# Four-layer graph network on one core: target rows and the scan's zero in a PSUM bank, sort steps pinned behind the messages, half runs as row groups in layer 2

## The chip, the cores and the metric

The kernel runs on one core of one Trainium2 chip. The core has five engines that run side by side and meet at semaphores: TensorE (PE in the profile, its weight loads PEld), VectorE (DVE), ScalarE (ACT), GpSimd (POOL) and SyncE (SP), which here only issues DMAs. SBUF is the working memory of 128 partitions; PSUM is a smaller memory of banks that TensorE writes and VectorE and ScalarE read. The metric is device time in microseconds (us); lower is better.

## The reference

A graph has 6250 nodes with 160 numbers each (64 scalars, 32 vectors of three components) and 100000 edges, sorted by their target node `dst`. Four layers follow one another, and each adds its result to the node rows:

```python
h = jnp.maximum(_layernorm(x, axis=-1), 0.0)
x = x + _L0_gnn_ref(h, node_vec1, src, dst, edge_attr_4, edge_attr_12, ...)
# the same frame for layers 1, 2 and 3; inside layers 0, 1 and 3:
h0, h1 = node-wise linear maps of h                  # scalars and vectors
w      = silu(edge_features @ W_fc1) @ W_fc2         # 192 weights for each edge
e0, e1 = h0[edge_src], h1[edge_src]                  # gather by source
mid_s  = concat(w0 * e0 * y0, w3 * dot(e1, y1))
mid_v  = concat((w1 * e0)[:, :, None] * y1[:, None, :], w2[:, :, None] * (e1 * y0))
ns, nv = segment_sum(mid_s, edge_dst), segment_sum(mid_v, edge_dst)
out    = node-wise linear maps of ns, nv, plus a linear map of h
```

Layer 2 has the directions turned around: it takes its node rows by `dst` and sums by `src`. Its messages must therefore be sorted by source first.

## The kernel before

Edges are handled in tiles of 128 (one edge per partition), four tiles to a group (`G = 4`), 28 tiles to a unit `u`, two windows of `WT = 14` tiles to a unit. There are 784 tiles (`TT`), 196 groups and 56 windows (`NW`) in every layer. A window's 14 tiles are two half runs of seven tiles, interleaved, so that tiles of even number belong to the first half and tiles of odd number to the second; each half touches fewer than 64 target nodes (`HN = 64`).

The program is `prologue()`, then `layers()`: `edges(0)`, `edges(1)`, `messages2()` and `sums2()` for layer 2, `edges(3)`. The order of instructions on each engine follows the order in which the Python code issues them, as a scheduler with a model of the engines rearranges it: an instruction that it sees ready may move ahead of earlier code that it sees waiting.

**Layers 0, 1 and 3 (`edges`).** For every group: `gather` (L1277) issues four indirect DMAs on POOL, each of which fetches 128 table rows by source into the tile `ge` (eight buffers, issued six groups ahead). `hidden` and `edge_weights` make the 192 weights per edge (matmuls L1266 or L1260, then L1300 or L1293; ScalarE evicts at L1304 and L1306 into `ws`). `messages` on VectorE makes the one-hot `oh` of targets (L1319: `iota` compared with `loc`) and the messages `msg` (L1330 to L1338). The matmul L1394 adds them up by target in the PSUM tile `pg`. At the end of a window, `nodes` takes the sums through `nodes_out` and `nodes_in` of the next layer, in small steps between the groups.

The tile `yls` (L1226) lies in a PSUM bank that VectorE alone uses. At the first group of a unit, L1313 copies three columns of the edges' directions into it, and L1330 and L1337 read them from there. The targets' rows `self.loc` are read from SBUF by L1319.

**The sort.** `positions()` is a generator that works out where each edge goes in source order: for each of the 54 buckets `b`, it makes `hit` (L1166), a running count `cum` with `tensor_tensor_scan` (L1168; its second input is `self.zeros_b`, a row of 784 zeros in SBUF), then multiplies (L1171) and adds into `pos` (L1172). Four steps come before the buckets, two steps belong to each bucket, one comes last. In layers 0 and 1, every third group asks for one step:

```python
            if li < 2 and i % 3 == 0:
                next(self.sort, None)
```

That is 66 steps in each of the two layers, of which 113 are needed.

**Layer 2, first part (`messages2`).** `select(k)` loads for window `k` 128 rows of the node table from the window's first node on (`tb`, L1443) and the targets of its 1792 edges, repeated on all partitions (`dt`, L1445, 896 KB), both through SP's queue; VectorE compares `dt` with each partition's node number `plus_w` (L1447) into the one-hot `oh`. In `messages`, the matmul L1479 (K = 128) picks each edge's row into the PSUM tile `pe`; ScalarE copies it out (L1484 to L1486); VectorE makes the message rows (L1497 to L1506); POOL scatters each tile's 128 rows to their sorted places in `rec2` (L1509; `row` has five buffers). `sums2` then reads `rec2` in order and adds up by source (L1611, L1613).

Of the kernel before, what the change touches and what calls it, by code (L numbers as in the profile page):

```python
# [11 lines left out]
F32 = mybir.dt.float32  # L12
BF16 = mybir.dt.bfloat16
I32 = mybir.dt.int32
AF = mybir.ActivationFunctionType
ALU = mybir.AluOpType
# [4 lines left out]
N = 6250  # L21
E = 100000
P = 128
# [9 lines left out]
G = 4  # L33
# [656 lines left out]
class Fast:  # L690
# [16 lines left out]
    def prologue(self):  # L707
# [119 lines left out]
        nc.tensor.matmul(pw[:, 2, :], lhsT=self.ones[0:1, :], rhs=wd[:, 3, :], start=True, stop=True)  # L827
        nc.vector.tensor_scalar(self.plus_w, pw[:, 0, :], iota_p, None, op0=ALU.add)

        column = pro.tile([P, NW], F32, name="column0")  # L830
        nc.vector.tensor_scalar(column, pw[:, 1, :], place, None, op0=ALU.add)
        other = pro.tile([P, NW], F32, name="other")
        nc.vector.tensor_tensor(other, column, pw[:, 2, :], ALU.not_equal)
# [308 lines left out]
    def positions(self, wk):  # L1142
# [21 lines left out]
        for b in range(BK + 1):  # L1164
            hit = wk.tile([P, TT], BF16, name="hit2", bufs=2)
            nc.vector.tensor_scalar(hit, self.src_b, float(b), None, op0=ALU.is_equal)  # L1166
            cum = wk.tile([P, TT], F32, name="cum", bufs=2)
            nc.vector.tensor_tensor_scan(cum, hit, self.zeros_b, self.off[:, b : b + 1], op0=ALU.add,  # L1168
                                         op1=ALU.add)
            yield  # L1170
            nc.vector.tensor_mul(cum, cum, hit)  # L1171
            nc.vector.tensor_add(pos, pos, cum)  # L1172
            yield
# [25 lines left out]

    def at(self, k, most=N):  # L1200

        return self.nc.values_load(self.first[0:1, 2 * k : 2 * k + 1], engines=[mybir.EngineType.SP], min_val=0, max_val=most,
                                   skip_runtime_bounds_check_because="a node's number")

    def edges(self, li):
# [19 lines left out]

        yls = p_y.tile([P, 2, 3, 2 * WT], F32, name="yls")  # L1226

# [81 lines left out]
        def messages(u, g):  # L1309
            n = width(u, g)  # L1310
            rt, yl = data[u][0], yls[:, u % 2]
            if g == 0:
                nc.vector.tensor_copy(yl, rt[:, :, 1:4].rearrange("p t c -> p c t"))  # L1313
            ws = wss.pop((u, g))[:, :n]
            ge = gath.pop((u, g))[:, :n]
            gs = slice(G * g, G * g + n)
            oh = wk.tile([P, G, HN], F32, name="oh", bufs=3)
            t0 = 2 * WT * u + G * g
            tt(oh[:, :n], self.iota[:, None, :HN].to_broadcast([P, n, HN]),  # L1319
               self.loc[:, t0 : t0 + n, None].to_broadcast([P, n, HN]), ALU.is_equal)  # L1320
            msg = wk.tile([P, G, AW + 64], F32, name="msg", bufs=3)[:, :n]
            mvec = msg[:, :, 0:288].rearrange("p g (c m) -> p g c m", c=3)
            e0 = ge[:, :, 0:64]
            e1 = ge[:, :, 64:160].rearrange("p g (c u) -> p g c u", c=3)
            yv = yl[:, :, gs].rearrange("p c t -> p t c")
            t1 = msg[:, :, AW : AW + 64]
# [10 lines left out]
            tt(mvec[:, :, :, 0:64], by3(t1, 64), yv[:, :, :, None].to_broadcast([P, n, 3, 64]), ALU.mult)  # L1337
            tt(mvec[:, :, :, 64:96], e1, by3(ws[:, :, 64:96], 32), ALU.mult)  # L1338
            return oh, msg

# [41 lines left out]
        for i, (u, g) in enumerate(groups):  # L1382
            prepare(i + AHEAD)
            weights_of(i + 2)
            if i + 1 < len(groups):
                edge_weights(*groups[i + 1])
            oh, msg = messages(u, g)
            for k in range(width(u, g)):
# [12 lines left out]
            if li < 2 and i % 3 == 0:  # L1401
                next(self.sort, None)
        for n in live:
# [7 lines left out]
    def messages2(self):  # L1411
# [26 lines left out]
        def select(k):  # L1438

            n = min(WT, TT - WT * k) * P  # L1440
            at = self.at(k)
            tb = ld.tile([P, 160], F32, name="tb")
            nc.sync.dma_start(tb, self.table[2][ds(at, P), :])  # L1443
            dt = ld.tile([P, WT * P], I32, name="dt", bufs=2)
            nc.sync.dma_start(dt[:, :n], self.a["dst_w"][k : k + 1, :n].to_broadcast([P, n]))  # L1445
            oh = ld.tile([P, WT, P], F32, name="oh", bufs=3)
            nc.vector.tensor_scalar(oh.rearrange("p t e -> p (t e)")[:, :n], dt[:, :n], self.plus_w[:, k : k + 1], None,  # L1447
                                    op0=ALU.is_equal)
            ohs[k] = tb, oh
# [22 lines left out]
        def messages(u, g):  # L1472
            n = width(u, g)
            t0 = 2 * WT * u + G * g
            ts = slice(t0, t0 + n)
            pe = p_e.tile([P, G, 256], F32, name="pe")
            for k in range(n):
                tb, oh = ohs[(t0 + k) // WT]
                nc.tensor.matmul(pe[:, k, :160], lhsT=oh[:, (t0 + k) % WT, :], rhs=tb, start=True, stop=True)  # L1479
            pw = pws.pop((u, g))[:, :n]  # L1480
            pe = pe[:, :n]
            row = wk.tile([P, G, RW], F32, name="row", bufs=5)[:, :n]
            ev = wk.tile([P, G, 224], F32, name="ev", bufs=3)[:, :n]
            nc.scalar.copy(ev[:, :, 0:160], pe[:, :, 0:160])  # L1484
            nc.scalar.copy(ev[:, :, 160:224], pe[:, :, 64:128])
            nc.scalar.copy(row[:, :, 294:390], pe[:, :, 64:160])  # L1486
            nc.scalar.copy(row[:, :, 256:262], self.edge_in[:, ts, :])
# [165 lines left out]
def _layout(inputs):  # L1653
# [46 lines left out]
    a["dst_t"] = by_tile(i["dst"], 1 << 20).T  # L1700
    a["dst_w"] = by_tile(i["dst"], 1 << 20).reshape(NW, WT * P)
    rec0 = np.zeros((E, 8), np.float32)
# [58 lines left out]
```

## Time and profile before

| | us |
|---|---|
| median of 3 runs | 6616.68 |
| the three runs | 6699.25, 6581.44, 6616.68 |
| the profiled execution, whole | 5448.67 |
| its span, first to last instruction | 5446.9 |

The profiled execution took 1168 us less than the median of the runs without a profile. What follows is about the profiled one; the stages are cut at the first and last indirect DMA of each:

| stage | us | what it is |
|---|---|---|
| 0 to 171 | 171 | prologue |
| 171 to 1265 | 1094 | gathers of layer 0 |
| 1265 to 1324 | 59 | from layer 0 to layer 1 |
| 1324 to 2395 | 1071 | gathers of layer 1 |
| 2395 to 2455 | 60 | from layer 1 to layer 2 |
| 2455 to 3550 | 1095 | scatters of layer 2 |
| 3550 to 4380 | 830 | sums of layer 2 |
| 4380 to 5420 | 1040 | gathers of layer 3 |
| 5420 to 5447 | 27 | end |

How to read it: "busy" of an engine is the time its instructions took, and a busy engine need not be the one that sets the end. An indirect DMA on POOL is an instruction in which POOL prepares the transfer; the transfer itself comes after it. "Idle before" is the time in which the engine had nothing running, put down to what ended it; "issue" means that the profile shows nothing that was waited for.

### The profile page before, as it was taken

The numbers are of one execution on the slowest core, as the hardware profiler recorded it, in microseconds if no ns is written. First come the engines' busy times: TensorE is split into PE (matmuls) and PEld (weight loads), VectorE is DVE, ScalarE is ACT, GpSimd is POOL, SyncE is SP. The second block draws the span as 40 slices with busy tenths as digits, with TensorE's granted clock in tenths as the row PEclk, the third lists the DMA queues.
The fourth block names the chain that finished last, engine by engine and source line by source line (L and its number), as shares of the span: only waits on it lengthen the run. The fifth ranks groups of instructions, "written<-read, shape, count | busy, mean of one in ns | idle before, by whom it ended". The sixth has DMA issues, their size and how long they took to land.

```text
span 5446.9 us, 77043 instructions
## 1 busy us (share of the span) xinstructions
PE 4624.0 (85%) x22084; PEld 2866.7 (53%) x22084; DVE 4217.8 (77%) x11655; ACT 2087.1 (38%) x6858; POOL 3346.0 (61%) x3143
## 2 busy tenths in 40 slices
PE   6799999997999999976666666689999988888887
PEld 4455555554555555544444444478888844444443
DVE  6688889888878897867777777767777767777777
ACT  5344444443544444533333333312222243343433
POOL 0577777774777777747777777700000067777776
PEclk9899999998989898987787877799999978788887
DMA  3333333322333333336666666477777533333332
GB/s 95 105 97 88 91 87 90 88 75 73 98 94 94 90 95 93 90 101 239 215 219 215 222 218 223 166 283 237 238 235 237 164 87 80 82 81 82 83 79 57
DMA packets 371211, 733.89 MB, mean 135 GB/s; under 512 B 69677, under 2 KB 249098, under 8 KB 370650
## 3 DMA queue, kind: packets, MB, share of 16 engines
q1 hardware_dynamic: 207122, 379.11, 22.3%
q0 software_dynamic: 163072, 349.43, 22.0%
q8 instruction: 180, 2.95, 0.2%
q14 instruction: 253, 2.07, 0.1%
q10 hardware_dynamic: 584, 0.33, 0.0%
HBM read 519.59 MB, written 209.08 MB: 134 GB/s over the span
## 4 chain that ended last, share of the span: by engine, by line
PE 52%; DVE 16%; DMA 14%; POOL 6%; issue 5%; ACT 3%; SPq 0%; DVEq 0%; ACTq 0%; POOLq 0%
PE pg L1394 12%; PE pg L1613 7%; DMA rec<-row,edge_to 7%; PE pw L1300 7%; DMA ge<-table,rt 6%; PE pg L1611 5%; POOL ge L1277 5%; PE ph L1266 4%; PE pa L1022 3%; PE pt_out L1062 2%; PE po L1082 2%; POOL rec L1509 2%; PE ph L1455 2%; DVE msg L1337 2%; PE pw L1293 2%
## 5 line engine op out<-in xcount | busy, mean ns | idle before, releaser
L1277 POOL DMA_INDIRECT ge<-table,rt x2352 | 2489.1, 1058 | 1774.1 <-DMA skip<-sk 830.3
L1394 PE MATMUL pg<-msg,oh 128*64 128x384 f32 x4704 | 1061.4, 572 | 165.6 <-DVE msg L1338 139.7
L1509 POOL DMA_INDIRECT rec<-row,edge_to x784 | 856.1, 1092 | 299.0 <-issue 191.2
L1304 ACT ACTIVATE ws<-pw,rt 128x96 f32<-128x96 f32 x2352 | 695.8, 348 | 820.5 <-DVE msg L1338 298.6
L1300 PE MATMUL pw<-w_w2y,hh 100*128 100x192 f32 x3136 | 673.5, 353 | 10.6 <-ACT ws L1306 7.7
L1394 PEld LDWEIGHTS pg<-msg,oh 128*64 128x64 f32 x4704 | 305.9, 150 | 709.0 <-issue 252.5
L1300 PEld LDWEIGHTS pw<-w_w2y,hh 100*128 100x128 f32 x3136 | 534.9, 202 | 236.9 <-ACT ws L1306 138.6
L1337 DVE TENSOR_TENSOR msg<-msg,yls 128x768 f32<-128x768 f32 x588 | 555.7, 945 | 0.0
L1613 PE MATMUL pg<-msg,oh 128*120 128x288 f32 x1668 | 541.5, 406 | 0.0
L1330 DVE TENSOR_TENSOR pr<-ge,yls 128x384 f32<-128x384 f32 x588 | 320.2, 545 | 220.7 <-DMA ge<-table,rt 219.9
L1269 ACT ACTIVATE hh<-ph 100x1024 f32<-100x1024 f32 (+1 forms) x336 | 269.1, 801 | 463.7 <-PE pw L1293 206.2
L1479 PE MATMUL pe<-tb,oh 128*128 128x160 f32 x1568 | 348.4, 363 | 112.5 <-ACT row L1486 112.3
L1266 PE MATMUL ph<-ft,w_w1r 12*100 12x512 f32 (+1 forms) x784 | 382.3, 658 | 71.2 <-ACT hh L1269 57.0
L1611 PE MATMUL pg<-rt,oh 128*120 128x192 f32 x1668 | 410.0, 328 | 29.3 <-DMA rt<-rec 29.3
L1479 PEld LDWEIGHTS pe<-tb,oh 128*128 128x128 f32 x1568 | 277.6, 226 | 274.5 <-ACT row L1486 221.9
L1333 DVE TENSOR_TENSOR msg<-ws,ge 128x512 f32<-128x512 f32 x588 | 402.0, 684 | 0.0
L1306 ACT COPY ws<-pw 128x192 f32<-128x192 f32 x1176 | 388.5, 330 | 0.0
L1455 PE MATMUL ph<-ft,w_w1d 128*128 128x512 f32 x224 | 162.4, 819 | 263.2 <-ACT hh L1457 262.4
L1502 DVE TENSOR_TENSOR row<-pw,ev 128x512 f32<-128x512 f32 x196 | 135.2, 690 | 301.8 <-ACT row L1488 298.3
L1611 PEld LDWEIGHTS pg<-rt,oh 128*120 128x120 f32 x1668 | 298.0, 184 | 117.6 <-issue 30.7
L1331 DVE TENSOR_REDUCE dot<-pr 128x128 f32<-128x384 f32 x588 | 344.2, 585 | 0.1
L1338 DVE TENSOR_TENSOR msg<-ge,ws 128x384 f32<-128x384 f32 x588 | 324.4, 552 | 0.0
(486 smaller groups left out, 7327.6 us busy)
## 6 DMA issues: line engine op xcount, KB each, us to landing
rt<-rec SPq DMA_DIRECT2D x208, 780.0 KB
dt<-in_dst_w_dram SPq DMA_DIRECT2D x56, 896.0 KB
ge<-table,rt POOLq DMA_INDIRECT x2352
ft<-in_ft_dram SPq DMA_DIRECT2D x56, 512.0 KB
ft<-in_ft_dram SPq DMA_DIRECT2D x28, 896.0 KB
xt<-x SPq DMA_DIRECT2D x168, 82.0 KB
rec<-row,edge_to POOLq DMA_INDIRECT x784
rt<-in_rec_dram SPq DMA_DIRECT2D x84, 112.0 KB
```

Of the source, the lines that this page charges most:

```text
L1266: nc.tensor.matmul(ph[:, i], lhsT=w1[r : r + K, :], rhs=ft[r : r + K, 4 * P * (j // 2) :][:, : 4 * P], start=True, stop=True)
L1277: nc.gpsimd.indirect_dma_start(out=ge[:, k, :], out_offset=None, in_=self.table[li], in_offset=bass.IndirectOffsetOnAxis(ap=rt[:, G * g + ...
L1300: nc.tensor.matmul(pw[:, i, :192], lhsT=hh[:, k + i, :], rhs=w2, start=True, stop=True)
L1304: nc.scalar.activation(ws[:, k0 + i, 0:96], pw[:, i, 0:96], AF.Copy, scale=rt[:, G * g + k0 + i, 0:1])
L1306: nc.scalar.copy(ws[:, k0 : k0 + m, 96:192], pw[:, :m, 96:192])
L1333: tt(msg[:, :, AW - 64 : AW + 64].rearrange("p g (k u) -> p g k u", k=2), ws.rearrange("p g (k u) -> p g k u", k=2)[:, :, :, 0:64], e0[:, ...
L1337: tt(mvec[:, :, :, 0:64], by3(t1, 64), yv[:, :, :, None].to_broadcast([P, n, 3, 64]), ALU.mult)
L1394: nc.tensor.matmul(pg[half], lhsT=oh[:, k, :], rhs=msg[:, k, :AW], start=t % WT < 2, stop=t % WT >= WT - 2)
L1479: nc.tensor.matmul(pe[:, k, :160], lhsT=oh[:, (t0 + k) % WT, :], rhs=tb, start=True, stop=True)
L1509: d = nc.gpsimd.indirect_dma_start(out=self.rec2, out_offset=bass.IndirectOffsetOnAxis(ap=self.edge_to[:, t0 + k : t0 + k + 1], axis=0), i ...
L1611: nc.tensor.matmul(pg[:, 0:192], lhsT=oh[:, k, :], rhs=rt[:, k, 0:192], start=first, stop=end, skip_group_check=True)
L1613: nc.tensor.matmul(pg[:, 192:480], lhsT=oh[:, k, :], rhs=msg[:, k, :], start=False, stop=end, skip_group_check=True)
```

## The change

1. The PSUM tile `yls` becomes part of a tile `bank`: two times four rows of 28 columns, and one column of zeros (`self.zero`), cleared once in each of the layers 0, 1 and 3. A second copy at the first group of a unit puts 28 columns of `self.loc` into the fourth row, and the one-hot of L1319 reads them there.
2. The scan of the sort takes `self.zero`, repeated 784 times, in place of `self.zeros_b`.
3. Each sort step is traced inside `tc.issue_after(last.ins)`, which adds an order on VectorE: the step's VectorE instructions stay behind the last message instruction of the group that asked for it.
4. In layer 2, `select` loads each half run's 64 table rows to partitions 0 to 63 or 64 to 127, and the targets of that half's 896 edges beside them. `oh` has 896 columns in place of 1792. The matmul that picks rows has K = 64, tiles of even number in partitions 0 to 63 and of odd number in 64 to 127, and their results go to the two halves of `pe`; ScalarE's copies put the tiles in order again. `plus_w` and the host's array `dst_w` are laid out to suit.

```diff
-        nc.vector.tensor_scalar(self.plus_w, pw[:, 0, :], iota_p, None, op0=ALU.add)
...
+        nc.vector.scalar_tensor_tensor(self.plus_w, column, -1.0, pw[:, 0, :], op0=ALU.add, op1=ALU.add)
...
-            nc.vector.tensor_tensor_scan(cum, hit, self.zeros_b, self.off[:, b : b + 1], op0=ALU.add,
+            nc.vector.tensor_tensor_scan(cum, hit, self.zero.to_broadcast([P, TT]), self.off[:, b : b + 1], op0=ALU.add,
                                          op1=ALU.add)
...
-        yls = p_y.tile([P, 2, 3, 2 * WT], F32, name="yls")
+        bank = p_y.tile([P, 8 * 2 * WT + 1], F32, name="bank")
+        yls = bank[:, : 8 * 2 * WT].rearrange("p (u c t) -> p u c t", u=2, c=4)
+        self.zero = bank[:, 8 * 2 * WT :]
+        nc.vector.memset(self.zero, 0.0)
...
-                nc.vector.tensor_copy(yl, rt[:, :, 1:4].rearrange("p t c -> p c t"))
+                nc.vector.tensor_copy(yl[:, 0:3], rt[:, :, 1:4].rearrange("p t c -> p c t"))
+                nc.vector.tensor_copy(yl[:, 3], self.loc[:, 2 * WT * u : 2 * WT * u + 2 * WT])
...
             tt(oh[:, :n], self.iota[:, None, :HN].to_broadcast([P, n, HN]),
-               self.loc[:, t0 : t0 + n, None].to_broadcast([P, n, HN]), ALU.is_equal)
+               yl[:, 3, gs, None].to_broadcast([P, n, HN]), ALU.is_equal)
...
-            tt(mvec[:, :, :, 64:96], e1, by3(ws[:, :, 64:96], 32), ALU.mult)
-            return oh, msg
+            last = tt(mvec[:, :, :, 64:96], e1, by3(ws[:, :, 64:96], 32), ALU.mult)
+            return oh, msg, last
...
             if li < 2 and i % 3 == 0:
-                next(self.sort, None)
+                with tc.issue_after(last.ins):
+                    next(self.sort, None)
...
-            n = min(WT, TT - WT * k) * P
-            at = self.at(k)
             tb = ld.tile([P, 160], F32, name="tb")
-            nc.sync.dma_start(tb, self.table[2][ds(at, P), :])
-            dt = ld.tile([P, WT * P], I32, name="dt", bufs=2)
-            nc.sync.dma_start(dt[:, :n], self.a["dst_w"][k : k + 1, :n].to_broadcast([P, n]))
-            oh = ld.tile([P, WT, P], F32, name="oh", bufs=3)
-            nc.vector.tensor_scalar(oh.rearrange("p t e -> p (t e)")[:, :n], dt[:, :n], self.plus_w[:, k : k + 1], None,
+            dt = ld.tile([P, WT // 2 * P], I32, name="dt", bufs=2)
+            for h in range(2):
+                rows = slice(HN * h, HN * h + HN)
+                nc.sync.dma_start(tb[rows], self.table[2][ds(self.at(k, half=h), HN), :])
+                nc.sync.dma_start(dt[rows], self.a["dst_w"][2 * k + h : 2 * k + h + 1, :].to_broadcast([HN, WT // 2 * P]))
+            oh = ld.tile([P, WT // 2, P], F32, name="oh", bufs=3)
+            nc.vector.tensor_scalar(oh.rearrange("p t e -> p (t e)"), dt, self.plus_w[:, k : k + 1], None,
                                     op0=ALU.is_equal)
...
             for k in range(n):
                 tb, oh = ohs[(t0 + k) // WT]
-                nc.tensor.matmul(pe[:, k, :160], lhsT=oh[:, (t0 + k) % WT, :], rhs=tb, start=True, stop=True)
+                h, rows = k % 2, slice(HN * (k % 2), HN * (k % 2) + HN)
+                nc.tensor.matmul(pe[:, 2 * h + k // 2, :160], lhsT=oh[rows, (t0 + k) % WT // 2, :], rhs=tb[rows],
+                                 start=True, stop=True)
...
-            nc.scalar.copy(ev[:, :, 0:160], pe[:, :, 0:160])
-            nc.scalar.copy(ev[:, :, 160:224], pe[:, :, 64:128])
-            nc.scalar.copy(row[:, :, 294:390], pe[:, :, 64:160])
+            nc.scalar.copy(pair(ev[:, :, 0:160]), pe[:, :, :, 0:160])
+            nc.scalar.copy(pair(ev[:, :, 160:224]), pe[:, :, :, 64:128])
+            nc.scalar.copy(pair(row[:, :, 294:390]), pe[:, :, :, 64:160])
```

More of the change, by code (lines that the diff above doesn't have):

```diff
@@ L1198, in layers, with at @@
         es.close()
-    def at(self, k, most=N):
-        return self.nc.values_load(self.first[0:1, 2 * k : 2 * k + 1], engines=[mybir.EngineType.SP], min_val=0, max_val=most,
+    def at(self, k, most=N, half=0):
+        return self.nc.values_load(self.first[0:1, 2 * k + half : 2 * k + half + 1], engines=[mybir.EngineType.SP], min_val=0, max_val=most,
                                    skip_runtime_bounds_check_because="a node's number")
@@ L1317, in messages @@
             oh = wk.tile([P, G, HN], F32, name="oh", bufs=3)
-            t0 = 2 * WT * u + G * g
             tt(oh[:, :n], self.iota[:, None, :HN].to_broadcast([P, n, HN]),
-               self.loc[:, t0 : t0 + n, None].to_broadcast([P, n, HN]), ALU.is_equal)
+               yl[:, 3, gs, None].to_broadcast([P, n, HN]), ALU.is_equal)
             msg = wk.tile([P, G, AW + 64], F32, name="msg", bufs=3)[:, :n]
@@ L1324, in messages @@
             e1 = ge[:, :, 64:160].rearrange("p g (c u) -> p g c u", c=3)
-            yv = yl[:, :, gs].rearrange("p c t -> p t c")
+            yv = yl[:, 0:3, gs].rearrange("p c t -> p t c")
             t1 = msg[:, :, AW : AW + 64]
@@ L1386, in edges @@
                 edge_weights(*groups[i + 1])
-            oh, msg = messages(u, g)
+            oh, msg, last = messages(u, g)
             for k in range(width(u, g)):
@@ L1478, in messages @@
                 tb, oh = ohs[(t0 + k) // WT]
-                nc.tensor.matmul(pe[:, k, :160], lhsT=oh[:, (t0 + k) % WT, :], rhs=tb, start=True, stop=True)
+                h, rows = k % 2, slice(HN * (k % 2), HN * (k % 2) + HN)
+                nc.tensor.matmul(pe[:, 2 * h + k // 2, :160], lhsT=oh[rows, (t0 + k) % WT // 2, :], rhs=tb[rows],
+                                 start=True, stop=True)
+            pe = pe.rearrange("p (h t) c -> p t h c", h=2)
+            pair = lambda v: v.rearrange("p (t h) c -> p t h c", h=2)
             pw = pws.pop((u, g))[:, :n]
-            pe = pe[:, :n]
             row = wk.tile([P, G, RW], F32, name="row", bufs=5)[:, :n]
             ev = wk.tile([P, G, 224], F32, name="ev", bufs=3)[:, :n]
-            nc.scalar.copy(ev[:, :, 0:160], pe[:, :, 0:160])
-            nc.scalar.copy(ev[:, :, 160:224], pe[:, :, 64:128])
-            nc.scalar.copy(row[:, :, 294:390], pe[:, :, 64:160])
+            nc.scalar.copy(pair(ev[:, :, 0:160]), pe[:, :, :, 0:160])
+            nc.scalar.copy(pair(ev[:, :, 160:224]), pe[:, :, :, 64:128])
+            nc.scalar.copy(pair(row[:, :, 294:390]), pe[:, :, :, 64:160])
             nc.scalar.copy(row[:, :, 256:262], self.edge_in[:, ts, :])
@@ L1700, in _layout @@
     a["dst_t"] = by_tile(i["dst"], 1 << 20).T
-    a["dst_w"] = by_tile(i["dst"], 1 << 20).reshape(NW, WT * P)
+    a["dst_w"] = np.append(i["dst"], np.full(TT * P - E, 1 << 20, np.int32)).reshape(2 * NW, WT // 2 * P)
     rec0 = np.zeros((E, 8), np.float32)
```

## The prediction

> **What bounds the kernel now.** I read the table of stretches first, cut at the first and last indirect DMA of each stage; then POOL's own rows in the parts of layer 1; then the waits of VectorE by layer; then the order of time around single stalls; last the chain of waits where layer 0 ends.
>
> ```profile
> 171.00:1265.00 1094.00, 1037.72 (x4968) 596.91 (x4970) 950.18 (x2616) 512.16 (x1596) 855.03 (x784) 0.92 0.35 90
> 1324.00:2395.00 1071.00, 1006.12 (x4666) 552.99 (x4666) 889.14 (x2535) 506.00 (x1700) 832.23 (x784) 0.91 0.35 92
> 2455.00:3550.00 1095.00, 699.30 (x3302) 470.03 (x3302) 778.18 (x1610) 373.32 (x1076) 855.85 (x784) 0.79 0.61 214
> 4380.00:5420.00 1040.00, 881.47 (x4223) 450.87 (x4222) 805.45 (x2363) 404.91 (x1452) 801.20 (x784) 0.83 0.32 81
> ```
>
> Columns: stretch, length, busy PE, PEld, DVE, ACT, POOL (instructions), granted clock, DMA share, GB/s. These are layers 0 and 1, the scatters of layer 2, and layer 3. POOL's 784 instructions have 0.30 us between them throughout (784 x 0.30 = 235, and 235 + 855 = 1090 of 1094 in layer 0): it never waits inside a stage. Undisturbed, a gather takes 0.946 us (the median of the L1277 rows), so the floor of a stage is 784 x 1.25 = 980 us. What lies above it is gathers stretched: 113, 91, 96 (its floor row is 0.97) and 60 us in the four stages.
>
> ```profile
> 700.28 0.95 POOL L1277 DMA_INDIRECT ge<-table,rt  x1 [0.30 <-issue]
> 700.45 0.94 DVE L1337 TENSOR_TENSOR msg<-msg,yls 128x768 f32<-128x768 f32 x1
> ...
> 707.57 1.85 DVE L1168 TENSOR_TENSOR_SCAN cum<-hit,off,zeros_b 128x784 f32<-128x784 bf16 x1
> ...
> 707.97 2.21 POOL L1277 DMA_INDIRECT ge<-table,rt  x1 [0.30 <-issue]
> ...
> 4437.50 0.41 DVE L1319 TENSOR_TENSOR oh<-iota,loc 128x256 f32<-128x256 f32 x1
> 4437.53 1.20 POOL L1277 DMA_INDIRECT ge<-table,rt  x1 [0.30 <-issue]
> ```
>
> In this order of time (start, us, engine), a gather that begins inside a VectorE instruction with two SBUF inputs (the scan, the one-hot) is longer by what is left of it: 1.26 us under the scan, 0.25 under the one-hot. Beside L1337, which reads `yls` in PSUM, it keeps its 0.95. So VectorE shuts POOL out while it has both inputs in SBUF.
>
> ```profile
> DVE pr L1330 <- DMA ge<-table,rt: 10.2, 2, 9.9
> ...
> DVE pr L1330 <- DMA ge<-table,rt: 65.6, 55, 3.7
> ...
> DVE pr L1330 <- DMA ge<-table,rt: 144.1, 70, 6.4
> ```
>
> These are the waits of VectorE for gathered rows in layers 0, 1 and 3 (us, times, longest). Layer 0 waits twice: POOL runs some 20 us ahead there (group 105: gathered at 764.5, first read at 790.4), so PE and VectorE pace it (PE 1038 of 1094). Layers 1 and 3 are paced by POOL (group 180: read 4.1 and 2.5 us after the gather instruction's end), and layer 2's scatters too: ACT waits 482 us there for POOL to free `row`.
>
> ```profile
> L1277 POOL DMA_INDIRECT ge<-table,rt x176 | 176.9, 1005 | 53.6 <-issue 46.0 <-DMA ge<-table,rt 2.4 <-DVE msg L1333 1.5
> ...
> L1277 POOL DMA_INDIRECT ge<-table,rt x370 | 414.1, 1119 | 112.7 <-issue 93.8 <-DVE msg L1333 4.3 <-DMA ge<-table,rt 4.3
> ...
> L1277 POOL DMA_INDIRECT ge<-table,rt x235 | 239.2, 1018 | 71.6 <-issue 59.1 <-DMA ge<-table,rt 2.1 <-DVE msg L1333 1.8
> ```
>
> This is layer 1 in three parts, 1330 to 1560, 1560 to 2085 and 2085 to 2395 (count, busy, mean ns). Scans run in the middle part alone, 16 of them; the mean rises from 1.01 to 1.119 there, 370 x 0.107 = 40 us, or 2.4 us for each bucket.
>
> ```profile
> 1291.23 1.76 DVE cum L1168
> ...
> 1294.28 1.76 DVE cum L1168
> ...
> 1301.49 1.76 DVE cum L1168
> 1303.25 0.04 DVE rstd L970
> 1303.30 1.76 DVE cum L1168
> ```
>
> In the chain of waits from layer 0 to layer 1, sort steps of layer 1 sit between the last nodes' small instructions; seven scans start between 1291 and 1320.
>
> **The change, part by part.** *A stall's price.* A gather begins every 1.31 us in layer 1's parts without scans. An instruction of length L is hit with chance L / 1.31 and costs L / 2 then: L x L / 2.62. For layer 3's four instructions with two SBUF inputs (L1333 0.684, L1338 0.552, L1319 0.415, L1336 0.284) that is 0.39 us a group, 77 us in 196 groups, against 60 measured; I use 0.8 of it.
>
> *One-hot from PSUM (1).* 0.415 gives 0.066 x 196 x 0.8 = 10 us a layer. Layer 3: -10. Layer 1: PE is busy 94% and has little room, so half, -5 (0 to -10). Layer 0: 0, since the 20 us lead hides POOL; with no lead, -10. The instruction itself keeps its length: L1330 with an input in PSUM takes 545 ns, L1338 with none 552, both for 384 elements. The added copy of 28 columns, 28 times a layer, lies between L1073's 0.16 us (4 columns) and L1313's 0.31 (84); at 0.2 that is 6 us of VectorE a layer. L1319 and all later messages of the group queue behind it, then L1394. In layers 1 and 3 the wait for rows covers it; in layer 0 (VectorE 950 of 1094) I count +3 (0 to +6). Clearing the zero: under 1 us.
>
> *Scan from PSUM (2).* By the same formula a bucket costs 1.30 (scan) + 2 x 0.36 (L1171, L1172 at 0.97) + 0.05 (`hit`) = 2.07, near the measured 2.4; the scan's part is 63%, or 1.5 us. If freed, a bucket in layer 1 costs 0.9. No row shows a scan with an input in PSUM. Its length could fall, if fetching the zeros holds it back, or grow; the nearest rows, L1330 and L1338, say neither, so I keep 1.84 us.
>
> *Pinned steps (3).* The steps run in layer 0's tail go to layer 1: 66 steps make 4 + 62, or 31 buckets, in layer 0 and 23 in layer 1 (16 + 7). Layer 1 pays 23 x 0.9 = 21 us in place of 40: -19; if the scan still shuts POOL out, 23 x 2.4 - 40 = +15. VectorE does 7 x 3.8 = 27 us more in layer 1, of 889 in 1071; what queues behind a step (2.1 us for `hit` and scan) is the next group's messages, whose rows POOL has not delivered earlier anyway. In layer 0 the steps follow the same messages as before: 0. The transition: sort pieces fill 19 us of its chain from 1288 to 1313. Not all comes back, since the small instructions wait for each other: from the node's L991 to L888, layer 0's end takes 11.9 us and layer 1's, with no sort, 2.8. I take -13; the ends are -9 (that one node's) and -19 (all).
>
> *Half runs (4).* L1447 takes 1.17 us 56 times. Half the columns cannot take less than half, 0.59, nor more than 1.17; taking some 0.2 us as fixed gives 0.70. Stalls at one scatter per 1.40 us and 0.8: 56 x 1.17 x 1.17 / 2.8 x 0.8 = 22 us now, 8 then: -14, straight off a stage that POOL paces. SP issues four loads a window in place of two, 112 more DMAs, each with its register read (about 0.34 us on SP by rows L1443, L1445), and its queue carries later `ft` loads behind them. A rule speaks against this: the Trainium skill, "DMA: Bandwidth & Descriptors", Rules for kernel authors, says two transfers to disjoint partition halves only serialize; at the 0.6 us to the first byte that its Specifications give for SP's path, 112 would be an estimated 67 us if exposed. The row decides: VectorE waited for `dt` once in the whole stage, 15.7 us at its start, and SP has some 20 us a window. I count 0, with +4 to -4 at the start, where SP's queue is the chain. For PE, "TensorEngine Tiling (Array Packing)", Theoretical Speedup, promises up to two times for K of 64: an estimated half of L1479's 343 us. PE is busy 699 of 1095 there and POOL is late, so that is worth 0; were PE the bound, it would be up to -170. ScalarE's reordered copies (696, 387, 507 ns) have 720 us of idle around them.
>
> *Sum* against the profiled 5448.67: layer 0 +3, transition -13, layer 1 -24, layer 2 -14, layer 3 -10, sums and prologue 0: **-58, so 5391 us, 1.1% less.** The runs' median is 1.214 times the profiled execution, and no trace shows where the 1168 us lie. I carry the ratio over: 6617 x 0.9894 = **6547 us**. The skill's "Advanced Engine Details and Errata", Clock Domains, has engine costs at 1.18 to 1.25 times in another power profile; no run here shows that.
>
> **The rivals.**
> - *The scan slows (slower).* Reading zeros in PSUM could lengthen L1168. All 54 scans stand in front of messages, 31 of them in layer 0, where VectorE's delay goes to PE's stalls. The gain is gone when a scan grows by 58 / 54 = 1.1 us, to 2.9; at twice its length (3.68) the sum is -58 + 99 = +41, 5490, or 6666. Against it: the scan takes 2.35 ns an element and L1171 1.24, so the fetch is hardly its limit.
> - *The change doesn't do it.* If `hit` and the offsets, both in SBUF, still shut POOL out, layer 1 gives +15 in place of -19: -24, 5425, or 6588. A median of 6617 from a slower PE alone would end near there too: layers 1 and 3 would lose their gains to PE (5415 and 6576 with the transition and half of layer 2 left).
> - *Layer 0 gains too.* If its 20 us lead is a result of the stalls and not of PE, it gains 10 (one-hot) + 31 x 1.5 = 56 us, less the +3 already there: 5335, or 6479. For: its POOL is stretched most. Against: ten us of waiting in 1119.
>
> **How the numbers follow.** Main case 0.52 (6500 to 6590); no freeing, or PE 0.19 (6565 to 6625); layer 0 too 0.18 (6420 to 6500); slower scan 0.11 (6620 to 6790). The runs shown spread over 1.8%, so the ends move out by that noise: 6410 to 6690. A measurement of this kernel tells about 2% from no change: below 6484 or above 6749. Most of the third case and a little of the first fall below, 0.18; half of the last, and noise, above, 0.08.
>
> **What would show it.** Right: mean of L1277 near 1.00 us in layer 3 and 1.03 in layer 1; no stretched gather inside L1168; no scan in the chain from layer 0 to 1, and that gap near 46 us; L1447 near 0.7 us and L1509 near 1.07; layer 0 within 10 us of 1094. Wrong: a scan well over 1.9 us, gathers still stretched beside it, VectorE waiting for `dt`, or layer 0 shorter by tens of us.

## The result: slower by 3.3%, and the profile after

| | us |
|---|---|
| before, median of 4 runs | 6624.6 (6581.44 to 6699.25) |
| after, median of 4 runs | 6820.73 (6818.53 to 6857.2) |
| after / before | 1.0329, interval 1.0273 to 1.0385 |
| after, span of its profiled execution | 6855.4 |

The prediction was 6547, 1.1% less than before. The kernel before takes about 5471 us in three of the jobs below and 6625 to 6871 us in this job and two later ones, with all kernels of a job moving together, and the profile of before that the prediction was read from belongs to the 5471 kind while its runs do not. So that profile cannot be subtracted from the one of after; I call the two kinds the 5471 jobs and the 6630 jobs, and take every ratio within a job.

This is after in the result's job, by the same table of stretches as before (stretch, length, busy PE, PEld, DVE, ACT, POOL, granted clock, which is the share of TensorE's full clock that the profile shows as granted, DMA share, GB/s): layers 0 and 1, the scatters of layer 2, layer 3.

```profile
172.00:1615.00 1443.00, 1214.42 (x4908) 682.05 (x4910) 949.46 (x2614) 504.93 (x1578) 782.31 (x784) 0.79 0.25 68
1674.00:3220.00 1546.00, 1166.34 (x4539) 632.34 (x4540) 893.87 (x2528) 487.52 (x1653) 778.13 (x784) 0.75 0.23 64
3304.00:4532.00 1228.00, 593.77 (x3298) 402.04 (x3298) 751.67 (x1608) 374.50 (x1073) 829.23 (x784) 0.68 0.50 171
5362.00:6804.00 1442.00, 1016.85 (x4118) 524.55 (x4120) 782.66 (x2328) 394.96 (x1416) 760.77 (x784) 0.71 0.22 58
```

POOL's 784 gathers of layer 1 need 778 + 235 us, and the stage lasts 1546: POOL waits for a third of it. No engine is busy for more than 85% of any of these stages. And this is the same program, after, run again in a 5471 job (its median there: 5486.71), the same stages and the end:

```profile
172.00:1301.00 1129.00, 1052.29 (x4910) 595.48 (x4912) 949.36 (x2616) 505.52 (x1580) 797.86 (x784) 0.91 0.34 87
1359.00:2433.00 1074.00, 1011.06 (x4584) 553.29 (x4585) 898.22 (x2542) 496.88 (x1672) 789.48 (x784) 0.90 0.36 92
2509.00:3566.00 1057.00, 610.97 (x3298) 414.28 (x3298) 753.09 (x1609) 365.19 (x1073) 818.06 (x784) 0.71 0.59 199
4397.00:5419.00 1022.00, 892.96 (x4118) 465.23 (x4120) 784.35 (x2326) 394.69 (x1415) 771.09 (x784) 0.82 0.33 82
5419.00:5471.00 52.00, 28.51 (x140) 14.56 (x136) 32.55 (x106) 11.44 (x41) 0.48 (x1) 0.73 0.05 13
```

VectorE's and ScalarE's busy times are the same to 2.6% in both; TensorE's grow by 15% in layers 0 and 1 with the lower clock, 162 us of layer 0's 314. The rest is waiting. Where VectorE waits (us, times, longest), first in the 5471 job, then in the result's:

```profile
DVE at L1073 <- ACT at L1069: 335.5, 128, 9.7
...
DVE ang L1115 <- PE po L1082: 85.7, 51, 2.7
...
DVE pr L1333 <- DMA ge<-table,rt: 39.7, 17, 8.8
```

```profile
DVE at L1073 <- ACT at L1069: 1113.1, 132, 19.3
```

L1073 is a small addition, 0.16 us, in `nodes_out`: TensorE turns the sums of a window (L1062), ScalarE copies them (L1069), VectorE adds (L1073), TensorE multiplies (L1082). All 11,742 instructions of VectorE stand in the same order in both profiles, however long one of them waits, so while VectorE stands at L1073 no message is made. Before, unchanged, was profiled in no 6630 job; how long it waits at L1073 there is not known. Three of ScalarE's seven largest waits in the result's profile are put down to nothing that the profile knows (226 waits and 1344 us of "remote" in all, none in the 5471 profiles):

```profile
ACT hh L1272 <- remote: 305.0, 46, 40.6
ACT row L1496 <- remote: 263.4, 38, 11.4
...
ACT at L1069 <- remote: 196.6, 30, 10.4
```

One such place in order of time (start, us, engine), in the result's job and in the 5471 job:

```profile
198.42 1.65 PE L1303 MATMUL pw<-w_w2y,hh 100*128 100x192 f32 x4 [6.76 <-ACT ws L1309]
...
226.29 0.57 ACT L1307 ACTIVATE ws<-pw,rt 128x96 f32<-128x96 f32 x2 [27.92 <-remote]
```

```profile
187.66 1.57 PE L1303 MATMUL pw<-w_w2y,hh 100*128 100x192 f32 x8
...
188.62 0.58 ACT L1307 ACTIVATE ws<-pw,rt 128x96 f32<-128x96 f32 x2 [2.03 <-PE pw L1303]
```

The same eviction starts beside its matmul in one and 26 us after the matmul's end in the other. The trace of the result's job holds half the semaphore records of the other (45,532 against 94,608), so it cannot name what released it. Set instruction against instruction, the two traces of this one program differ by 1385 us. Following the lag from one to the next, some 215 ScalarE instructions that read what TensorE wrote are where it jumps by over 1.5 us, by 925 us together (4.3 us each), and 344 us build up in small steps on TensorE.

### The profile page after: what moved, and what is told of

Same layout as the page of the kernel before. It is cut to its first block, busy times and chain, and to the rows that moved or that the text cites. A ratio compares the mean times of both kernels' runs of the same rounds, so it can differ in the third digit from the quotient of the medians.

```text
span 6855.4 us, 77520 instructions
## 1 busy us (share of the span) xinstructions
PE 5037.3 (73%) x22084; PEld 3064.4 (45%) x22084; DVE 4198.2 (61%) x11742; ACT 2081.6 (30%) x6858; POOL 3153.0 (46%) x3143
## 5 line engine op out<-in xcount | busy, mean ns | idle before, releaser
L1280 POOL DMA_INDIRECT ge<-table,rt x2352 | 2322.7, 988 | 3168.5 <-DVE turn L1349 878.1
L1397 PE MATMUL pg<-msg,oh 128*64 128x384 f32 x4704 | 1199.1, 636 | 170.5 <-DVE msg L1341 81.6
L1517 POOL DMA_INDIRECT rec<-row,edge_to x784 | 829.6, 1058 | 482.2 <-issue 282.8
L1303 PE MATMUL pw<-w_w2y,hh 100*128 100x192 f32 x3136 | 766.7, 390 | 130.6 <-ACT ws L1309 116.1
L1303 PEld LDWEIGHTS pw<-w_w2y,hh 100*128 100x128 f32 x3136 | 616.7, 228 | 388.6 <-ACT ws L1309 190.1
L1073 DVE TENSOR_TENSOR at<-at 96x4 f32<-96x4 f32 x165 | 27.0, 164 | 1190.4 <-ACT at L1069 1113.1
L1397 PEld LDWEIGHTS pg<-msg,oh 128*64 128x64 f32 x4704 | 335.5, 165 | 817.1 <-issue 464.6
L1269 PE MATMUL ph<-ft,w_w1r 12*100 12x512 f32 (+1 forms) x784 | 474.2, 760 | 197.4 <-ACT hh L1272 95.6
L1485 PE MATMUL pe<-tb,oh 64*128 64x160 f32 x1568 | 272.0, 406 | 395.0 <-ACT row L1494 223.0
L1340 DVE TENSOR_TENSOR msg<-msg,bank 128x768 f32<-128x768 f32 x588 | 554.7, 943 | 0.0
L1485 PEld LDWEIGHTS pe<-tb,oh 64*128 64x128 f32 x1568 | 204.4, 252 | 547.2 <-ACT row L1494 307.7
L1296 PE MATMUL pw<-w_w2d,hh 64*128 64x192 f32 x1568 | 309.9, 429 | 45.6 <-ACT ws L1309 38.2
```

The lines of the kernel that those rows point to most:

```text
L1269: nc.tensor.matmul(ph[:, i], lhsT=w1[r : r + K, :], rhs=ft[r : r + K, 4 * P * (j // 2) :][:, : 4 * P], start=True, stop=True)
L1280: nc.gpsimd.indirect_dma_start(out=ge[:, k, :], out_offset=None, in_=self.table[li], in_offset=bass.IndirectOffsetOnAxis(ap=rt[:, G * g + ...
L1296: nc.tensor.matmul(pw[:, i, :192], lhsT=hh[r : r + 64, i, :], rhs=w2[r : r + 64, :], start=True, stop=True)
L1303: nc.tensor.matmul(pw[:, i, :192], lhsT=hh[:, k + i, :], rhs=w2, start=True, stop=True)
L1397: nc.tensor.matmul(pg[half], lhsT=oh[:, k, :], rhs=msg[:, k, :AW], start=t % WT < 2, stop=t % WT >= WT - 2)
L1485: nc.tensor.matmul(pe[:, 2 * h + k // 2, :160], lhsT=oh[rows, (t0 + k) % WT // 2, :], rhs=tb[rows], start=True, stop=True)
```

## The experiments

Every ratio is to the kernel before in the same job. Stages are from one profiled execution each, in us. Executions of one kernel spread by 0.8% (5443.56 to 5485.88 in 35 runs of before), so a stage's 15 us counts only where several kernels repeat it.

| kernel | 0 | 0 to 1 | 1 | 1 to 2 | 2, scatters | 3 | end |
|---|---|---|---|---|---|---|---|
| before, 5471 job | 1103 | 70 | 1073 | 61 | 1095 | 1047 | 27 |
| parts 1 + 2 | 1126 | 66 | 1076 | 69 | 1100 | 1020 | 50 |
| part 3 | 1115 | 57 | 1088 | 61 | 1094 | 1047 | 26 |
| part 4 | 1103 | 73 | 1068 | 60 | 1061 | 1048 | 27 |
| after, 5471 job | 1129 | 58 | 1074 | 77 | 1057 | 1023 | 51 |
| part 4, two cuts | 1099 | 55 | 1067 | 58 | 1058 | 1041 | 28 |
| before, late copy, 6630 job | 1362 | 83 | 1377 | 91 | 1238 | 1287 | 61 |
| after, late copy, 6630 job | 1411 | 60 | 1483 | 95 | 1211 | 1374 | 53 |
| after, result's job | 1444 | 58 | 1546 | 84 | 1228 | 1442 | 51 |

**Parts alone.** The first question was what the profile had left out; the second, which part costs. The first run is before, unchanged.

> The kernel before, unchanged, profiled a second time. The profile shown took 5448.67 us at a clock of 0.881 while its runs took 6617. Theory A (the shown profile is the exception): this one takes 6580 to 6700 us at a clock of 0.77 to 0.80, like the runs, and POOL waits inside the stages for free `ge` buffers as it does in the changed kernel (L0, L1 and L3 each 250 us or more longer than in the shown profile). Theory B (a profile of this kernel is faster than its runs): again about 5450 us, POOL without gaps, and the profile of the changed kernel with its gaps of 420, 530 and 440 us is what the change did.

Profile 5477.86, clock 0.877, and its 35 unprofiled runs have a median of 5470.73. So a profile does not make this kernel faster: in such a job it takes 5471 with or without one.

Parts 1 and 2 together (`bank` with `self.loc` and the zero):

```diff
-               self.loc[:, t0 : t0 + n, None].to_broadcast([P, n, HN]), ALU.is_equal)
+               yl[:, 3, gs, None].to_broadcast([P, n, HN]), ALU.is_equal)
...
-            nc.vector.tensor_tensor_scan(cum, hit, self.zeros_b, ...
+            nc.vector.tensor_tensor_scan(cum, hit, self.zero.to_broadcast([P, TT]), ...
```

> Parts 1 and 2 alone: one-hot and scan read from the PSUM bank, sort steps not pinned, layer 2 as before. Theory order (the changed code made the scheduler lay the node work of layers 0, 1 and 3 into the queues at worse places, and every engine stands in order behind it): slower by 1.5 to 3%, about 100 to 200 us, in layers 0, 1 and 3. Theory pinning (sort steps behind the messages delay what follows): within 0.7% of before, since nothing is pinned. Theory half runs (TensorE's K of 64 lowers the clock or slows layer 2): within 0.7% of before.

Measured: 5507.52, ratio 1.0066 (1.0046 to 1.0087). The parts that free POOL make the kernel slower. POOL is freed all the same: beyond the 0.305 us that always lie between two gathers it now waits 89, 44 and 5 us in layers 0, 1 and 3, where in before it had waited 4, 0 and 0.

Part 3 alone:

```diff
-                next(self.sort, None)
+                with tc.issue_after(last.ins):
+                    next(self.sort, None)
```

> Part 3 alone: the sort steps of layers 0 and 1 are pinned behind the group's last message instruction. Theory pinning: slower by 2 to 3% (130 to 200 us), all in layers 0 and 1. Theory order: between 0 and +2%, in layers 0 and 1 and perhaps 3, where the order on the engines also differs. Theory half runs: within 0.7%.

Measured: 5483.13, 1.0024 (1.0012 to 1.0037). The transition falls from 70 to 57 us as forecast, and layers 0 and 1 give it back (+13, +15).

Part 4 alone (`select`, L1479 and the copies, as in the diff above):

```diff
-            dt = ld.tile([P, WT * P], I32, name="dt", bufs=2)
+            dt = ld.tile([P, WT // 2 * P], I32, name="dt", bufs=2)
+            for h in range(2):
```

> Part 4 alone: half runs as row groups in layer 2. My forecast gave -14 us of 5449, so about -0.3%. Theory half runs: slower by 2 to 3%, in layer 2 or at a clock lower by 0.02 or more. Theories order and pinning: within 0.7% of before in layers 0, 1 and 2, with layer 3 between -1% and +1% of the whole because its order on the engines differs too.

Measured: 5431.34, 0.9921 (0.99 to 0.9942). The only part that pays: layer 2's scatters go from 1095 to 1061, all else stays.

**After, and after less one part.** The first is after unchanged, beside before in a 5471 job; the next leaves part 3 out, the last leaves part 4 out (each by the diff's own lines taken back).

```diff
-                with tc.issue_after(last.ins):
-                    next(self.sort, None)
+                next(self.sort, None)
```

> The changed kernel once more, beside new runs of the kernel before. Theory parts (the three parts add up, as measured singly: +0.66%, +0.24% and -0.79%): where the kernel before takes about 5470 us this one takes 5440 to 5520 us, within 0.7% of it; where the kernel before takes about 6620 us, the 3.3% comes back. Theory interaction (the complete change has an order of its own on the engines that is worse than any part's): slower by 2% or more, also where the kernel before takes 5470 us. In both, the mean of the gathers in layers 1 and 3 is 0.06 us or more shorter than before, so POOL is freed, and the granted clock says whether TensorE is idle more often.

> The change without part 3 (sort steps not pinned). Theory parts: 0.2% faster than the complete change. Theory interaction through the pinned steps: faster than the complete change by 1.5% or more if the 3.3% shows in this job.

> The change without part 4 (layer 2 as before). Theory parts: 0.8% slower than the complete change, so about +0.9% on the kernel before. Theory half runs (K of 64 lets TensorE idle more and its clock fall): faster than the complete change by 1% or more where the kernel before takes 6620 us.

Measured: after 5486.71, 1.0038 (1.0009 to 1.0067); without the pin 5458.76, 0.9976 (0.9961 to 0.9991); without half runs 5538.11, 1.0122 (1.0084 to 1.0161). So in a 5471 job the change as a whole is a wash: half runs give 0.8%, the PSUM bank and the pin take 1.2% between them. Beside the bank the pin is not needed: without it the transition takes 56 us, with it 58, and the kernel is 0.5% faster. The 3.3% of the result is not a property of the program alone.

**What in part 1 costs.** Part 1 alone, and then its added copy alone: 28 columns of `self.loc` are copied to the bank and the one-hot still reads SBUF.

```diff
+                nc.vector.tensor_copy(yl[:, 3], self.loc[:, 2 * WT * u : 2 * WT * u + 2 * WT])
...
                self.loc[:, t0 : t0 + n, None].to_broadcast([P, n, HN]), ALU.is_equal)
```

> Part 1 alone: the one-hot reads the targets' rows from the PSUM bank, with the added copy of 28 columns; the scan as before. Parts 1 and 2 together measured +0.66% and lengthened layer 0 by 23 us. Theory pace (TensorE and the node chain pace the layers, so freeing POOL buys nothing; what is added to VectorE is paid): +0.2 to +0.5%; the gathers' mean falls by 0.02 to 0.05 us, layer 3's gathers end 20 us earlier and the end after them is 20 us longer. Theory scan (the scan from PSUM is what slows layer 0): within 0.15% of before, layer 0 within 5 us of 1103.

> The added copy of 28 columns alone: it is made, but the one-hot goes on reading SBUF, so POOL is not freed. Theory pace with the copy as the price: +0.2 to +0.5%, as with part 1. Theory freed POOL (POOL running ahead is itself what disturbs the others, through memory or through the clock): within 0.15% of before, while part 1 alone is slower by 0.3% or more.

Measured: part 1 5491.06, 1.0039 (1.0023 to 1.0055); the copy 5469.71, 0.9994 (0.9981 to 1.0007). The copy costs nothing; the one-hot that reads the bank does, by freeing POOL or by the order of instructions that comes with it.

The order of instructions in the traces shows a second effect of the edits. The scheduler lays out TensorE, ScalarE and VectorE anew: of TensorE's 22,084 matmuls, three quarters stand at the same place in after as in before. I counted the places where fewer than five of the edges' matmuls lie on TensorE between turning a window's sums (L1062) and the next product (L1080 or L1082), which needs their result by way of ScalarE and VectorE: 18 in before, 18 with part 4, 20 with part 3, 27 with part 1, 32 with parts 1 + 2, 33 in after. But the copy alone has 25 and costs nothing, so their number is not the price. To take such short hops away, the node step is cut at two places, so that groups lie between:

```diff
         nc.sync.dma_start(to(self.table[li], 0), tb[rows])
+        yield
...
             nc.scalar.copy(at, pt)
+        yield
```

> Part 4 alone (measured -0.79%) with the node chain given more room: between ScalarE's copy of the turned sums and VectorE's addition to it, and between the table row's copy and the additions to the node row, the step is cut in two, so that VectorE's instruction comes half a group later in its queue. Theory pace: VectorE's wait for ScalarE at that addition, 57 to 90 us a layer, falls by half or more, and the kernel is 0.3% to 1.5% faster than part 4 alone. Theory POOL (POOL paces layers 1 and 3, as forecast): layers 1 and 3 within 5 us of 1068 and 1048.

> Parts 1, 2 and 4 with the same cut in the node chain. Without it, parts 1 and 2 cost 0.55% on top of part 4. Theory pace: with the chain out of the way POOL would pace, so parts 1 and 2 now pay: faster than part 4 with the cut by 0.3% or more, POOL waiting less than 100 us in the three layers. Theory POOL or theory scan: slower than part 4 with the cut by 0.3% or more, as without it.

With part 4: 5407.37, 0.9876 (0.986 to 0.9893), short hops 4. With parts 1, 2 and 4: 5401.25, 0.9866 (0.9842 to 0.9889), short hops 6. The bank's cost is gone: with the cuts, parts 1 + 2 cost no more (5401 against 5407), where without them they cost 0.55% (0.9976 against 0.9921). So in the 5471 jobs the bank's price hangs on where the node steps stand, and POOL's running ahead is not what costs. The forecast gain of 0.3% from the bank did not come, though, and VectorE's wait at the addition did not fall by half: it went from 204 to 186 us with part 4, and from 346 to 285 with parts 1, 2 and 4. Its other three waits in the node steps (L1041, L1095 and L1115 of before) fell more, from 133 to 39 and from 203 to 44 us together, and one (L1004) rose, from 15 to 32 and from 4 to 60. These two kernels beat before and after there.

**The other condition.** To bring the 5471 kind near the result, ScalarE's copy L1069 was to be made late: one column of the sums goes through a sigmoid first, which makes ScalarE change its table (361 table loads of 1.28 us in the trace, where before has 4), and is overwritten by the copy.

```diff
+            nc.scalar.activation(acc[:, 0:1], pg[:, 0:1], AF.Sigmoid)
             nc.scalar.copy(acc, pg)
```

> The kernel before with ScalarE made late on purpose: at each window's end in layers 0, 1 and 3 one column of the sums goes first through a sigmoid into the tile that the copy then fills, so that ScalarE's function tables are switched there and back again (336 switches; a table load takes 1.28 us in the profile, so 430 us or more of ScalarE's time just where TensorE's sums and the hidden layer wait for it). In the job where the change was 3.3% slower, the changed kernel's ScalarE instructions that wait for TensorE came late. All theories: slower than before by 2 to 12%. Its result is the base for the next run.

> The changed kernel with the same late ScalarE. Theory sensitivity (with POOL freed, VectorE waits for ScalarE's copy of the turned sums where it waited for gathered rows, so lateness of ScalarE goes straight to the end): 1.5% or more slower than the kernel before with late ScalarE. Theory no sensitivity: within 1% of it, and the 3.3% of the first job has another cause, which stays open.

> Part 4 alone with the same late ScalarE. Theory sensitivity through parts 1 to 3: 0.5 to 1.1% faster than the kernel before with late ScalarE, as without lateness. Sensitivity through part 4 (ScalarE's reordered copies and the lower clock in layer 2): slower than it by 0.5% or more.

> A better version: parts 1, 2 and 4 with the two cuts in the node chain, and a third before layer 1's two products of the node's hidden row, for which VectorE waited 60 us. Theory pace: 0.2 to 0.8% faster than with two cuts (0.9866 of before). Otherwise within 0.2% of it.

The job turned out to be of the 6630 kind (before: 6636.46). Before with late copies 6501.89, 0.9767 (0.9699 to 0.9835); after 6712.6, 1.0106 (1.0033 to 1.0178); part 4 6507.2, 0.9791 (0.9729 to 0.9852); parts 1, 2 and 4 with a third cut, ahead of `hk`, 6717.54, 1.0122 (1.0098 to 1.0146). The first and the last expectation failed: the extra work made before faster, and three cuts, of which two won in a 5471 job, lose here. The second came out as the theory of sensitivity has it, 3.2% between the two kernels with late copies; part 4 is neither faster nor slower (1.0008).

The first failure probably has its reason in the order again. Between the last messages ahead of TensorE's L1062 and L1073, VectorE has one group of messages (counted by L1337) in 53 or 54 of a layer's 55 windows, in before, in after and in each part alone. With the late copies the scheduler put two groups there in 14, 24 and 26 windows of layers 0, 1 and 3, in before and with part 4 (4, 14 and 26 in after). The wait at L1073 follows, first in before's version, then in after's:

```profile
DVE at L1073 <- ACT at L1069: 270.8, 93, 14.2
```

```profile
DVE at L1073 <- ACT at L1069: 794.1, 114, 20.1
```

The ratio after / before is 1.032 here too (6712.6 / 6501.89), and part 4 / before is 1.0008. So with late copies parts 1 to 3, not part 4, bring the 3%, though the two orders differ as well (64 windows with two groups against 44). POOL is no pacemaker here in any of them: before and part 4 with late copies, whose gathers are stretched as ever, leave it waiting 247 to 323 us in each of the three layers.

Then two groups everywhere, by three cuts between L1069 and L1073, and the scan alone (part 2; the bank's fourth row is not filled and the one-hot reads SBUF):

```diff
             nc.scalar.copy(at, pt)
+        yield
+        yield
+        yield
```

> The changed kernel with the node chain one group looser: between ScalarE's copy of the turned sums and VectorE's addition to it the generator gives way three times more, so that two groups of messages, not one, stand between the last messages before TensorE's turning matmul and VectorE's addition. Theory chain (VectorE's wait for ScalarE at that addition is where the freed time went, and where a late ScalarE strikes): 1.2% or more faster than the changed kernel on the same condition, so at most 0.992 of the kernel before where that takes 5470 us, and at most 1.015 of it where that takes 6630 us; the wait at the addition falls below 100 us (5470) or 350 us (6630). Theory other bound: within 0.5% of the changed kernel (1.004 or 1.033).

> Part 4 alone with the same looser chain. Theory chain: 0.5 to 2% faster than part 4 alone (0.992 where the kernel before takes 5470 us), and faster than the kernel before by 2% or more where that takes 6630 us, since the late-ScalarE kernels, in which a third of the windows had two groups between, were 2.3% faster there. It should be within 0.5% of the changed kernel with the looser chain, since POOL and TensorE then pace. Theory other bound: within 0.5% of part 4 alone.

> Part 2 alone: the scan reads its zero from PSUM. Parts 1 and 2 gave +0.66%, part 1 alone +0.39%. Theory pace: +0.1 to +0.4% where the kernel before takes 5470 us, with gathers in layer 1 shorter by 15 to 25 us and the stage no shorter. My forecast for it alone: -0.3% (19 us in layer 1, 0 in layer 0). Where the kernel before takes 6630 us, theory chain has it slower by 1 to 2.5%.

Before took 6871.04 in this job. After with two groups: 6728.66, 0.9777 (0.971 to 0.9845); part 4 with two groups: 6689.86, 0.9713 (0.9668 to 0.9759); the scan: 6879.8, 1.0025 (0.9999 to 1.0052). VectorE's waits of after with two groups (the line numbers are three higher from L1073 on), then of the scan:

```profile
DVE xt L1098 <- PE po L1085: 250.3, 43, 18.9
...
DVE at L1076 <- ACT at L1069: 188.2, 44, 15.1
```

```profile
DVE at L1073 <- ACT at L1069: 1034.2, 128, 17.5
```

This points to the order, and not the arithmetic, as what carries most of the result: after, 3.3% slower than before in the result's job, is 2.2% faster in this one once VectorE has two groups to do before it needs ScalarE. Neither after nor part 4 was run unchanged in this job, so what the two groups alone give here was not measured. Of what parts 1 to 3 cost beside part 4, 3.2% in the job ahead (6712.6 / 6507.2), 0.6% is left (6728.66 / 6689.86, intervals that overlap). Against too simple a reading: the scan's kernel waits 1034 us at L1073, nearly as long as after, and is only 0.25% slower than before, where the theory of the chain had 1 to 2.5%. Either before waits there as long, or the size of that wait does not decide. Parts 1 and 3 were not run alone in a 6630 job, so which of them costs there is open.

## Why the prediction was wrong

**The step that failed is "Layers 1 and 3 are paced by POOL", with what was built on it: "In layers 1 and 3 the wait for rows covers it", and the gains of 24 and 10 us.** I read from POOL's rows that it never waits, and from waits of VectorE for rows that POOL sets the pace. Both lines were true, but a stream that never waits is not yet the one that sets the end, and VectorE waited for rows in only 55 of layer 1's 196 groups. In the same view of before, layer 1, a longer wait stands above the line that I quoted:

```profile
DVE at L1073 <- ACT at L1069: 90.7, 34, 10.1
...
DVE pr L1330 <- DMA ge<-table,rt: 65.6, 55, 3.7
```

Take POOL's stalls away, and in a 5471 job it waits 92 us in layer 0, 46 in layer 1 and 12 in layer 3 (in the result's job 422, 529 and 442), beyond the 0.305 us between gathers. The terms of my sum, forecast and then as the 5471 profiles of before and after have them: layer 0 +3 and +26; transition -13 and -12; layer 1 -24 and +1; the way to layer 2 0 and +15; layer 2 -14 and -38; layer 3 -10 and -24, but with its end +24. (These two profiles differ by -5 us, the medians of the runs by +16.) All four kernels with parts 1 and 2 and without cuts repeat layer 3's -24 to -27 and the end's +23 or +24: the gathers end sooner, and the node work left over at the end is longer by as much. With the two cuts the end is back at 26 us. These are VectorE's waits of before in the whole kernel, 5471 job, to set beside those of after:

```profile
DVE pr L1330 <- DMA ge<-table,rt: 225.4, 131, 8.8
DVE at L1073 <- ACT at L1069: 212.4, 87, 8.5
...
DVE ang L1115 <- PE po L1082: 32.3, 23, 2.8
```

The wait for rows fell by 186 us, and the other two, in the node steps, rose by 177. A wait took the place of the one removed, a case that I did not price. In layers 0 and 1 TensorE is busy 93 to 95% in both kernels, which I had used for half of one gain only.

**The second failed step is "I carry the ratio over".** The profile did not belong to the runs, and the condition changes which order wins: after is 1.0038 in the one and 1.0329 in the other, the cut version of parts 1, 2 and 4 0.9866 with two cuts in the one, 1.0122 with three in the other. In the 5471 job the sum was off by 1.4% (forecast -1.1%, measured +0.4%). The other 2.9% of the miss come with the condition, as far as the runs with late copies show through parts 1 to 3. What makes ScalarE late there is not shown, and stays open. Another power profile, which I had named, does not fit: VectorE's and ScalarE's busy times are the same in both kinds of job. The kind may go with the chip: the record has the 5471 jobs on chips 7, 9 and 1 and the later 6630 jobs on chips 14 and 15, and does not name that of the result's job.

**What held.** *POOL is freed.* In this stretch of after, in the 5471 job, a gather begins inside the scan and keeps its 0.95 us:

```profile
1372.59 1.84 DVE L1168 TENSOR_TENSOR_SCAN cum<-hit,off,bank 128x784 f32<-128x784 bf16 x1
1373.08 0.94 POOL L1280 DMA_INDIRECT ge<-table,rt  x1 [0.30 <-issue]
1374.33 0.95 POOL L1280 DMA_INDIRECT ge<-table,rt  x1 [0.30 <-issue]
```

In before 44 gathers begin inside a scan, mean 2.05 us; in after 80, mean 0.945. The mean gather is 1.007 us in layer 1 (forecast 1.03) and 0.985 in layer 3 (1.00). The scan itself stays at 1.84 us (medians 1.839 and 1.836): the rival of the slower scan is out, and with it my only case on the slower side. So are "the change doesn't do it" and "layer 0 gains too".

*The transition* fell by 12 or 13 us with the pin (forecast 13), and scans per layer went from 28 / 16, with 8 between, to 30 / 23 and 1. (With part 3 alone this one is still in the chain of waits.) The pin does this alone, but so does part 2: the scan's kernel and parts 1, 2 and 4 without the pin have 30 / 23 and 1 as well. The time came back inside the layers, where the +3 and 0 for VectorE's added work were too small.

*Layer 2* had the right mechanism and too small a size: -34 with part 4 alone, forecast -14. The one-hot and the scatters, of before and of after in 5471 jobs (count, busy, mean ns, idle before):

```profile
L1509 POOL DMA_INDIRECT rec<-row,edge_to x784 | 855.0, 1091 | 301.2 <-issue 189.5 <-DVE row L1505 66.2 <-DVE row L1502 15.2
...
L1447 DVE TENSOR_SCALAR oh<-dt,plus_w 128x1792 f32<-128x1792 int32 x56 | 64.9, 1158 | 14.4 <-DMA dt<-in_dst_w_dram 14.3
```

```profile
L1517 POOL DMA_INDIRECT rec<-row,edge_to x784 | 818.3, 1044 | 315.1 <-issue 185.2 <-DMA dt<-in_dst_w_dram 76.6 <-DVE row L1513 8.8
...
L1451 DVE TENSOR_SCALAR oh<-dt,plus_w 128x896 f32<-128x896 int32 x56 | 38.4, 686 | 0.0
```

L1447's 0.70 was right, and so was what it costs the scatters: 22 us of stretching forecast and 23 measured (about 50 scatters by 0.45 us), then 8 forecast and 3 measured. The term left out is stretching under other VectorE instructions, some 14 us less too. The reading against the Trainium skill's rule on partition halves ("DMA: Bandwidth & Descriptors", Rules for kernel authors) held as well: 112 more loads cost nothing that can be seen, and with part 4 the start of layer 2 took 60 us against 61. For TensorE the half runs bring something, though less than the half I estimated (before, then after, in 5471 jobs):

```profile
L1479 PE MATMUL pe<-tb,oh 128*128 128x160 f32 x1544 | 338.6, 359 | 109.4 <-ACT row L1486 108.9
```

```profile
L1485 PE MATMUL pe<-tb,oh 64*128 64x160 f32 x1540 | 272.0, 411 | 192.4 <-ACT row L1494 190.2
```

One matmul with K = 64 takes longer, with the clock down from 0.80 to 0.71, but they overlap more, so that TensorE is busy with them 272 us in place of 339. That the stage got no shorter by it was right: TensorE is not the bound there.

## What to carry to other kernels

An engine without idle time is the pacemaker only if the others would be idle less when it speeds up: before counting its stalls as time, find the next wait, which in a program with in-order engines can be a short hop over three of them whose distance a scheduler chose. After each edit compare the order of instructions, since it may change with the edit and cost more than the edit saves, and set the distance of such hops by hand. Where the profile and the runs differ by a fifth, forecast both conditions or widen the range to cover a change of order between them; a ratio is not carried over for free.

## What the hardware showed unexpectedly

The granted clock is the page's row of tenths, of after in the result's job and then in a 5471 job (40 slices of the span):

```profile
PEclk9788887778777777777676676679999766776777
```

```profile
PEclk9988999998889888996777776699999978888887
```

At a finer grain it was only 1.0 or 0.5, in stretches that are multiples of 3.41 us. In the 3.41 us before it halved TensorE was busy 51% on average in before and 56% in after (5471 jobs), 39% in after in the result's job; in those before it came back, 99%. Half clock held for 1344, 1516 and 3088 us of the three. The Trainium skill, "TensorE: Matmul & The Clock Gate", What's actually happening, gives two states and a window of 3413 ns; the trace agrees, and shows that a gap need not fill a window to lose the clock: in the 5471 profile of after, 160 of the 210 falls had no idle gap of that length in the 6.8 us before. The two kinds of job differ in the traces themselves: every profile of a 5471 job holds 92,500 to 94,600 semaphore records, every one of a 6630 job 44,300 to 48,900. In the sums of layer 2 the clock was 0.98 in all runs, and that stage took 829 to 833 us in both. It is the stages with many hops between TensorE, ScalarE and VectorE that lengthen in the 6630 jobs. A lower clock explains some of it, as TensorE's busy time shows; it can also be a result of the waits, and no run here tells the two apart.
